# Two attention layers and four feed-forward passes on one core: q's and k's preparation cut into one-engine pieces, and begun earlier, with the next chunk's first row maxima moved to the end of chunk 0

## The chip, the core and the metric

One core of a Trainium2 chip. The metric is device time in microseconds (us) of one run of the whole program. Lower is better. Instructions run on TensorE (PE; its weight loads are shown as PEld), VectorE (DVE), ScalarE (ACT), GpSimd (POOL), and SyncE (SP), which here only issues DMAs. Each engine takes its own instructions strictly in the order in which the program lists them; semaphores make one wait for another.

## The reference: what is computed

The input x is 2048 positions by 256 features. A layer is x += 0.5 FFN(LN(x)); x += Attention(LN(x)); x += 0.5 FFN(LN(x)). There are two layers, so the stages are f0, attention 0, f1, f2, attention 1, f3, and each stage has its LayerNorm ahead. Layer 0's FFN has ternary weights and an RMS norm, layer 1's keeps the two largest of every four hidden values. Both attentions are causal, with 16 heads of 16 features:

```
q, k, v = LN(x) @ Wq, LN(x) @ Wk, LN(x) @ Wv         # layer 1: + bias
layer 1: q, k = q*cos + swap(q)*sin, k*cos + swap(k)*sin     # rotary
scores = q @ k^T / 4 (+ a position bias in layer 0), causal
x += softmax(scores) @ v @ Wo                        # layer 1: + bias
```

## The kernel before, in words

**Tiling.** x lies as features by positions, in four chunks of 512 positions (chunk c, `CH` = 512). A feed-forward stage goes through the chunks, and for each through eight hidden blocks f = 0..7 (L444 to L468): gate and up matmuls (`gate_up`, L281, or L306 in layer 0), Silu on ACT (L317), a product on DVE (L318), then in layer 1 the 2-of-4 choice (`sparsify`, DVE and POOL, L387 to L418) and the down matmuls (L292), which for a chunk are issued beside blocks 4 and 5 of the next chunk. After every block, `feed_forwards` calls `beside(s, at, f)` (L468), where `at` counts the chunks.

**Attention.** Heads go in four groups of four for each chunk of queries: group n = 4c + g. A *slot* is one pair (group n, key block kb of 128 keys); chunk c has 4(c+1) slots for each of its groups, so chunk 0 has slots 0 to 15, chunk 1 slots 16 to 47, chunk 2 slots 48 to 95. In a slot PE makes the transposed scores `pst` (L733, and the mask L741), ACT takes their exponential (L753, tile `pT`), and PE sums `pav` with the values (L768). The exponential needs the row maximum beforehand, folded into q as three more rows: so for a later group PE makes the scores the other way round, `pq` (L671, and the mask L679), and DVE reduces each to a maximum `mx` (L682). One *unit* (n, t, kc) is four such score blocks for 128 queries t against chunk kc of keys. When a group's units are done, `mx_end` (L689, L694) makes the negated maximum on DVE, and one slot later `mx_turn` (L699) transposes it on PE (`ptm`, L704), copies it on ACT (`qx`, L712) and stores it by three DMAs into three rows of the group's q tile (L714), for which that group's `pst` waits. PSUM has two pairs of banks for `pst`, and three single ones (`ps_one`) which `pq`, `pp`, `pv`, `ptm` share.

**Preparation.** `prep_qk(c, what)` (L521) is a generator; a *piece* runs from one yield to the next. It makes q or k of chunk c: matmuls `pp` for two halves (L536), in layer 0 a bf16 copy on ACT (L544) and the rest on DVE (L545), in layer 1 bias on ACT (L547, tile `dn`). Layer 1 then has the halves of `dn` swapped by two DMAs into `sw` (L556), multiplies `dn` by the cosine on DVE (L571) and `sw` by the sine on POOL (L575, two instructions), adds (DVE, L577), copies the bf16 part (ACT, L578) and subtracts it (DVE, L579). Both layers go on with the second part (ACT, L580) and third part (POOL, L581), and six DMAs to a scratch in DRAM (L585). Before the change, all of L577 to L585 is one piece. `prep_v` has two pieces of matmuls `pv` (L598) with the copies to `va` (ACT L609 in layer 0, DVE L611 in layer 1). `load` (L636) brings a group's k and q back from the scratch to SBUF (L640, L645).

**What sets the order.** There is no list scheduler for PE, ACT, DVE and POOL: they get their instructions in the order in which the Python code issues them. SP's DMAs are placed by a planner. Chunk 0's preparation is drawn from `beside0` and `beside1` (L1023, L1030), one piece a block, beside the last chunk of f0 and the last one and a half of f2. Chunk 1's is drawn by `step()` (L877) after each of the seven units ahead of slot 0 (the *opening*, L912 to L916), then once a slot; chunk c+1's, once a slot in chunk 1 and in every second slot in chunk 2 (L975). If a `load` wants what is not there, `need` (L880) draws all pieces up to it at once. `put` (L837) says in which slot a unit is issued (L846 to L859), `uses` and `load_to` (L900 to L908) load each group three slots ahead of its first unit.

Of the kernel before, what the change touches and what calls it, by code (L numbers as in the profile page):

```python
# [26 lines left out]
G = 4  # L27
F = 1024
FC = F // P
CH = 512  # L30
NCH = S // CH
# [15 lines left out]
def macaron_kernel(ctx: ExitStack, tc: tile.TileContext, a, out):  # L47
# [13 lines left out]
    def ps_one(name):  # L61
        return ps3.tile([P, CH], F32, tag="one", name=name)
# [124 lines left out]
    def draw(work):  # L187
        while work and next(work[0], "end") == "end":
            work.popleft()
# [7 lines left out]
    def ready(c):  # L197

        while pending[c]:
            pull()  # L200
# [289 lines left out]
    def attention(layer, following):  # L490
# [9 lines left out]
        with ExitStack() as st:  # L500
# [20 lines left out]
            def prep_qk(c, what):  # L521

                ready(c)
                if what == "k" and c > 0:
                    nc.gpsimd.memset(va[c], 1.0)
                at = 0 if what == "q" else DC
                name = f"{layer}_{what}{c}"
                dn = ka.tile([P, DC, CH], F32, tag="dn", bufs=2 - layer, name=f"dn{name}")
                pt = [
                    ka.tile([P, DC, CH], BF16, tag=f"part{j}", bufs=1, name=f"p{j}{name}")  # L530
                    for j in range(3)
                ]
                for i in range(DC):
                    pp = ps_one(f"pp{name}_{i}")
                    for dc in range(DC):
                        nc.tensor.matmul(  # L536
                            pp,
                            lhsT=wqkv[:, dc, (at + i) * P : (at + i + 1) * P],
                            rhs=xns[c][:, dc, :],
                            start=dc == 0,  # L540
                            stop=dc == DC - 1,
                        )
                    if layer == 0:
                        nc.scalar.copy(pt[0][:, i, :], pp)  # L544
                        nc.vector.tensor_tensor(dn[:, i, :], pp, pt[0][:, i, :], ALU.subtract)  # L545
                    else:
                        nc.scalar.activation(  # L547
                            dn[:, i, :], pp, AF.Identity, bias=b_qk[:, at + i : at + i + 1]
                        )
                    if i == 0:  # L550
                        yield
                if layer == 1:

                    sw = ka.tile([P, DC, CH], F32, tag="sw", bufs=1, name=f"sw_{what}{c}")
                    for o in range(2):
                        nc.sync.dma_start(  # L556
                            out=sw[o * 64 : o * 64 + 64, :, :],
                            in_=dn[64 - o * 64 : 128 - o * 64, :, :],
                        )
                    if turns.get("of") != c:  # L560
                        turns["of"] = c
                        turns["cs"] = ka.tile(
                            [P, 2, CH], F32, tag="cs", bufs=1, name=f"cs_{what}{c}"
                        )
                        nc.sync.dma_start(
                            out=turns["cs"], in_=a["cos_sin"][:, :, c * CH : (c + 1) * CH]
                        )
                    cs = turns["cs"]
                    yield
                    yield  # L570
                    nc.vector.tensor_tensor(  # L571
                        dn, dn, cs[:, 0:1, :].to_broadcast([P, DC, CH]), ALU.mult
                    )
                    for i in range(DC):
                        nc.gpsimd.tensor_tensor(sw[:, i, :], sw[:, i, :], cs[:, 1, :], ALU.mult)  # L575
                    yield
                    nc.vector.tensor_tensor(dn, dn, sw, ALU.add)  # L577
                    nc.scalar.copy(pt[0], dn)  # L578
                    nc.vector.tensor_tensor(dn, dn, pt[0], ALU.subtract)  # L579
                nc.scalar.copy(pt[1], dn)  # L580
                nc.gpsimd.tensor_tensor(pt[2], dn, pt[1], ALU.subtract)  # L581
                for j in range(3):
                    for m, part in enumerate(Q_PARTS if what == "q" else K_PARTS):
                        if part == j:
                            nc.sync.dma_start(  # L585
                                out=parts[what, c][:, m, :, :].rearrange("i p t -> p i t"),
                                in_=pt[j],
                            )
                done.add((what, c))
                yield  # L590

            def prep_v(c):
                ready(c)
# [24 lines left out]
            def first():  # L618
                nc.gpsimd.memset(va[0], 1.0)
                yield  # L620
                for work in (prep_qk(0, "k"), prep_qk(0, "q"), prep_v(0)):
                    yield from work
# [207 lines left out]
            first = []  # L830
# [3 lines left out]
            LEAD = 3  # L834
            maxima = {}

            def put(slot, n, t, kc):  # L837
                maxima.setdefault(max(slot, -1), []).append((n, t, kc))

            def whole(n):  # L840

                return [(n, t, kc) for kc in range(n // G) for t in range(T)] + [(n, 3, n // G)]
# [8 lines left out]
            for c in range(NCH):  # L851
                units = [u for n in groups[c * G + 1 : (c + 1) * G + 1] for u in whole(n)]
                places = [i for i, (n, kb) in enumerate(slots) if n // G == c and kb <= c * T]
                if c == 0:
                    places = range(first[G] - LEAD)
                if c == NCH - 1:
                    places = [i for i in places if slots[i][0] < groups[-1]]
                for j, u in enumerate(units):
                    put(places[j * len(places) // len(units)], *u)  # L859
# [7 lines left out]
            def run_due(all_of=False):  # L867
                while True:
                    due = [x for x in later if all_of or x[0] <= now[0]]
                    if not due:  # L870
                        return
                    later.remove(due[0])
                    due[0][1](*due[0][2])
# [3 lines left out]
            def step():  # L877
                draw(preps)
# [11 lines left out]
            def mx_next(unit, heads):  # L890
                n, t, kc = unit
                mx_unit(n, t, kc, heads)
                if 3 in heads:
                    left[n] -= 1
                    if not left[n]:
                        mx_end(n)
                        at(1, mx_turn, n)
# [11 lines left out]

            load_to(-1)  # L910
            preps.extend((prep_qk(1, "k"), prep_qk(1, "q"), prep_v(1)))
            for unit in maxima[-1]:  # L912
                mx_next(unit, (0, 1, 2, 3))
                step()
                now[0] += 1
                run_due()  # L916

# [21 lines left out]
            for i, (n, kb) in enumerate(slots):  # L939
                c = n // G  # L940
                if kb == 0 and n % G == 0 and 0 < c < NCH - 1:

                    preps.extend((prep_qk(c + 1, "k"), prep_qk(c + 1, "q"), prep_v(c + 1)))
# [3 lines left out]
                units = maxima.get(i, [])  # L947
# [69 lines left out]
    begun = []  # L1017

    def begin(layer, following):
        att = attention(layer, following)  # L1020
        begun[:] = att, next(att)

    def beside0(s, at, f):  # L1023
        if not quants and not begun:
            raw_scope.close()
            begin(0, "f1")
        if at == NCH - 1:
            next(begun[1], None)

    def beside1(s, at, f):  # L1030
        if s == 1 and at == 0 and f == FC // 2:
            own.close()
            ffn0_scope.close()
            begin(1, "f3")
        if s == 1 and (at == NCH - 1 or at == NCH - 2 and f >= FC // 2):
            next(begun[1], None)

    def attend():
        att, first = begun
# [15 lines left out]
    attn_w = {0: load_attn(0)}  # L1055
    w1 = None
    feed_forwards([(0, "f0", range(NCH))], beside0)
    attend()
    attn_w[1] = load_attn(1)
# [5 lines left out]
    w1 = (wgu1, wd1)  # L1065
# [5 lines left out]
    own = ExitStack()  # L1071
    own0 = own.enter_context(tc.tile_pool(name="own0", bufs=1, side="right"))
    feed_forwards([(0, "f1", range(NCH)), (1, "f2", range(NCH))], beside1, own0)
    attend()
    feed_forwards([(1, "f3", range(NCH))], lambda s, at, f: None)
# [95 lines left out]
```

## Time and profile before

| what | us |
|---|---|
| runs | 1935.06, 1936.63, 1938.12 (median 1936.63) |
| the profiled execution | 1938.73 (its span 1936.7) |
| PE busy | 1735.6 (90%) |
| DVE, ACT, POOL busy | 1353.1 (70%), 884.7 (46%), 456.9 (24%) |
| f2's last down matmul ends, attention 1's first `pq` starts | 1161.8, 1168.1 |
| first `pst` of chunk 0, 1, 2, 3 in attention 0 | 267.1, 323.1, 442.8, 606.2 |
| the same in attention 1 | 1196.1, 1267.2, 1397.5, 1568.2 |

The lines of the profile give start, duration, engine, source line, operation, output<-inputs and shapes; in brackets the time for which the engine stood idle just before, and what ended it. The rows by stretch give, for each engine, its busy time and in brackets its number of instructions, in the order PE, PEld, DVE, ACT, POOL, then the granted PE clock (1.00 is full, 0.50 half), the share of the DMA engines, and GB/s. The first `pst` of a chunk is found by counting: each slot has four L733 matmuls, an attention 160 slots.

### The profile page before, as it was taken

To read this page: it belongs to the slowest core of one execution; us is meant where nothing else is said; L and a number is where in the kernel's file an instruction comes from. 1 tells how busy PE (TensorE), PEld (TensorE's weight loads), DVE (VectorE), ACT (ScalarE), POOL (GpSimd) and SP (SyncE) were. 2 spreads that over 40 slices of the span, in tenths; PEclk is the share of its full clock that TensorE was granted. 3 is DMA by queue.
4 is the path that set the end of the run, shared out by engine and by line. 5 is a ranking of instruction groups with operands and counts; after the bars stand their busy time and mean duration, and the time that the engine had idled before them with its cause. 6 is when DMAs were issued, how large, how long until landed. Compare 5 with 4: busy or idle time off the path is not lost. (4 is left out here: it accounts for less than half of the span.)

```text
span 1936.7 us, 26968 instructions
## 1 busy us (share of the span) xinstructions
PE 1735.6 (90%) x10659; PEld 747.2 (39%) x10684; DVE 1353.1 (70%) x2384; ACT 884.7 (46%) x1112; POOL 456.9 (24%) x418
## 2 busy tenths in 40 slices
PE   5699788999999999789999875888998999999997
PEld 1233344443434443233444332433434344433443
DVE  7866378787788883666566655867867888826654
ACT  4243244555556668334432312444555656673220
POOL 3455321101000000455444432211111000004322
PEclk9799899999999999989999987998999999999998
DMA  4001252212211010200000115323122110000000
GB/s 130 1 1 33 79 154 72 85 55 82 74 55 46 28 28 1 74 1 0 1 12 0 54 44 153 104 73 97 52 70 87 43 43 27 18 2 0 11 11 22
DMA packets 50511, 93.10 MB, mean 48 GB/s; under 512 B 5425, under 2 KB 33073, under 8 KB 50129
## 3 DMA queue, kind: packets, MB, share of 16 engines
q1 hardware_dynamic: 49296, 89.28, 15.3%
q10 hardware_dynamic: 1088, 2.10, 0.3%
q8 instruction: 84, 1.38, 0.3%
q14 instruction: 43, 0.34, 0.1%
HBM read 59.51 MB, written 27.26 MB: 45 GB/s over the span
## 5 line engine op out<-in xcount | busy, mean ns | idle before, releaser
L682 DVE TENSOR_REDUCE mx<-pq 128x1 f32<-128x512 f32 (+3 forms) x1280 | 697.6, 602 | 146.0 <-PE pq L679 86.8
L753 ACT ACTIVATE pT<-pst 128x1024 f32<-128x1024 f32 (+3 forms) x614 | 533.1, 895 | 319.9 <-PE pst L733 166.4
L671 PE MATMUL pq<-k,q 105*128 105x512 bf16 (+7 forms) x1280 | 386.9, 351 | 76.9 <-DVE mx L682 55.3
L733 PE MATMUL pst<-q,k 99*128 99x512 bf16 (+7 forms) x1280 | 354.9, 351 | 5.1 <-ACT pT L753 4.3
L768 PE MATMUL pav<-pT,va 128*32 128x256 f32 (+1 forms) x4608 | 326.2, 379 | 5.2 <-DVE yt L789 5.0
L281 PE MATMUL pg_f<-xn,wgu 128*128 128x512 f32 x512 | 229.6, 602 | 11.5 <-DVE hr_f L318 11.5
L794 POOL TENSOR_TENSOR zt<-yt,rd 128x64 f32<-128x64 f32 x128 | 38.3, 299 | 774.4 <-DVE rd L793 774.3
L733 PEld LDWEIGHTS <-k 105*128 105x128 bf16 (+1 forms) x1280 | 111.0, 98 | 229.4 <-issue 165.2
L317 ACT ACTIVATE sl_f<-pg_f 128x512 f32<-128x512 f32 x128 | 76.0, 594 | 251.2 <-PE pg_f L281 174.9
L671 PEld LDWEIGHTS <-q 105*128 105x128 bf16 (+1 forms) x1280 | 124.0, 99 | 146.8 <-issue 44.3
L768 PEld LDWEIGHTS pav<-pT,va 128*32 128x32 f32 x4608 | 106.6, 109 | 190.9 <-issue 136.1
L306 PE MATMUL pg_f<-xn,wgu 128*128 128x512 bf16 x500 | 154.0, 413 | 20.8 <-DVE wgu L170 6.8
L281 PEld LDWEIGHTS pg_f<-xn,wgu 128*128 128x128 f32 x512 | 98.6, 193 | 136.9 <-issue 121.0
L306 PEld LDWEIGHTS <-wgu 128*128 128x128 bf16 x768 | 77.3, 101 | 167.1 <-issue 73.1
L292 PE MATMUL po_f<-h_f,wd 128*128 128x512 f32 x256 | 117.4, 613 | 17.3 <-DVE h_f L418 17.3
L340 POOL TENSOR_TENSOR ss_f<-ss_f,sq_f 128x512 f32<-128x512 f32 x56 | 90.5, 1615 | 110.7 <-ACT sq_f L339 110.5
L679 PE MATMUL pq<-mask_qk,ident_b 128*128 128x128 bf16 x512 | 107.0, 226 | 0.0
L741 PE MATMUL pst<-mask_kq,ident_b 128*128 128x128 bf16 x512 | 102.7, 221 | 0.0
L318 DVE TENSOR_TENSOR h_f<-sl_f,pg_f 128x512 f32<-128x512 f32 x64 | 43.6, 681 | 77.4 <-ACT sl_f L317 76.9
L306 PE MATMUL pg_f<-xm_f,wgu 128*128 128x512 bf16 x253 | 83.4, 411 | 14.8 <-DVE xm_f L238 14.3
L789 DVE STREAM_TRANSPOSE yt<-pav 128x128 f32<-128x128 f32 x128 | 39.7, 310 | 76.8 <-PE pav L768 76.8
L394 DVE TENSOR_TENSOR ge_f<-h_f 128x1536 bf16<-128x1536 f32 (+2 forms) x48 | 67.6, 1437 | 28.0 <-ACT h_f L387 28.0
(132 smaller groups left out, 1798.3 us busy)
## 6 DMA issues: line engine op xcount, KB each, us to landing
k<-dk SPq DMA_DIRECT2D x80, 384.0 KB
dk<-p_k SPq DMA_DIRECT2D x48, 256.0 KB
dq<-p_q SPq DMA_DIRECT2D x48, 256.0 KB
q<-dq SPq DMA_DIRECT2D x32, 384.0 KB
x<-in_xT ACTq DMA_DIRECT2D x4, 512.0 KB
raw<-in_w_gu SPq DMA_DIRECT2D x8, 256.0 KB
wgu<-in_w_gu SPq DMA_DIRECT2D x1, 2048.0 KB
cs_k<-in_cos_sin SPq DMA_DIRECT2D x4, 512.0 KB
```

Source lines behind the costliest of these rows:

```text
L281: nc.tensor.matmul(pg[:, half, :], lhsT=wgu[:, dc, half * F + f * P : half * F + (f + 1) * P], rhs=xn[:, dc, :], start=dc == 0, stop=dc == ...
L292: nc.tensor.matmul(po, lhsT=w[:, f, dc * P : (dc + 1) * P], rhs=h[:, f, :], start=f == 0, stop=f == FC - 1,)
L306: nc.tensor.matmul(pg[:, half, :], lhsT=wgu0[:, dc, half * F + f * P : half * F + (f + 1) * P], rhs=xp[part][:, dc, :], start=part == 0 an ...
L317: nc.scalar.activation(sl, pg[:, 0, :], AF.Silu)
L340: nc.gpsimd.tensor_tensor(ss, ss, sq, ALU.add)
L671: nc.tensor.matmul(pq, lhsT=qs[n][0:rows, hh, t * P : (t + 1) * P], rhs=ks[n, kc][0:rows, hh, 0:w], start=True, stop=kc < c,)
L679: nc.tensor.matmul(pq[:, w - P : w], lhsT=ident_b, rhs=mask_qk, start=False, stop=True)
L682: nc.vector.tensor_reduce(mxs[n][:, t, hh, kc : kc + 1], pq, AX.X, ALU.max)
L733: nc.tensor.matmul(ps[i][:, lo:CH], lhsT=ks[n, kc][0:rows, hh, t * P : (t + 1) * P], rhs=qs[n][0:rows, hh, lo:CH], start=True, stop=kc < c,)
L741: nc.tensor.matmul(ps[i][:, lo : lo + P], lhsT=ident_b, rhs=mask_kq, start=False, stop=True)
L753: nc.scalar.activation(pT[:, :, lo:CH], pair[:, :, lo:CH], AF.Exp, scale=0.25)
L768: nc.tensor.matmul(acc[hh * SLOT : (hh + 1) * SLOT, a:b], lhsT=va[kc][:, t, v0 : v0 + SLOT], rhs=pTs[hh // 2][:, hh % 2, a:b], start=kb == ...
```

## The change

It cuts `prep_qk` at four more places (a piece then holds instructions of one compute engine, save for the multiply with POOL's two and the copy with POOL's subtraction), and drops its last yield, so that the six DMAs to the scratch run in one call with the next generator's first piece. Chunk 0's preparation is begun four blocks earlier in f0 as well, and in f2's last chunk two pieces are drawn a block. In layer 1's opening, two pieces are drawn after each unit. In chunk 0, a group's last unit goes to the first slot of the group before it, and the five units of group 4 that were spread from slot 4 on come to slots 9 to 13.

```diff
--- before.py
+++ after.py
@@ -575,10 +575,14 @@
                         nc.gpsimd.tensor_tensor(sw[:, i, :], sw[:, i, :], cs[:, 1, :], ALU.mult)
                     yield
                     nc.vector.tensor_tensor(dn, dn, sw, ALU.add)
+                    yield
                     nc.scalar.copy(pt[0], dn)
+                    yield
                     nc.vector.tensor_tensor(dn, dn, pt[0], ALU.subtract)
+                yield
                 nc.scalar.copy(pt[1], dn)
                 nc.gpsimd.tensor_tensor(pt[2], dn, pt[1], ALU.subtract)
+                yield
                 for j in range(3):
                     for m, part in enumerate(Q_PARTS if what == "q" else K_PARTS):
                         if part == j:
@@ -587,7 +591,6 @@
                                 in_=pt[j],
                             )
                 done.add((what, c))
-                yield
 
             def prep_v(c):
                 ready(c)
@@ -852,7 +855,10 @@
                 units = [u for n in groups[c * G + 1 : (c + 1) * G + 1] for u in whole(n)]
                 places = [i for i, (n, kb) in enumerate(slots) if n // G == c and kb <= c * T]
                 if c == 0:
-                    places = range(first[G] - LEAD)
+
+                    for j, u in enumerate(units):
+                        put(first[u[0] - 1] if u[0] < G else first[G - 1] - 6 + j, *u)
+                    continue
                 if c == NCH - 1:
                     places = [i for i in places if slots[i][0] < groups[-1]]
                 for j, u in enumerate(units):
@@ -911,7 +917,8 @@
             preps.extend((prep_qk(1, "k"), prep_qk(1, "q"), prep_v(1)))
             for unit in maxima[-1]:
                 mx_next(unit, (0, 1, 2, 3))
-                step()
+                for _ in range(1 + layer):
+                    step()
                 now[0] += 1
                 run_due()
 
@@ -1020,20 +1027,25 @@
         att = attention(layer, following)
         begun[:] = att, next(att)
 
+    def go_on(at, f):
+        if at == NCH - 1 or at == NCH - 2 and f >= FC // 2:
+            next(begun[1], None)
+            if w1 and at == NCH - 1:
+                next(begun[1], None)
+
     def beside0(s, at, f):
         if not quants and not begun:
             raw_scope.close()
             begin(0, "f1")
-        if at == NCH - 1:
-            next(begun[1], None)
+        go_on(at, f)
 
     def beside1(s, at, f):
         if s == 1 and at == 0 and f == FC // 2:
             own.close()
             ffn0_scope.close()
             begin(1, "f3")
-        if s == 1 and (at == NCH - 1 or at == NCH - 2 and f >= FC // 2):
-            next(begun[1], None)
+        if s == 1:
+            go_on(at, f)
 
     def attend():
         att, first = begun
```

Line numbers after the change: up to L577 as before; the copy, the subtraction, the second copy and POOL's subtraction come to L579, L581, L583 and L584, the DMAs to the scratch to L589; from there to the placing of units three more (L598, L671, L682, L714, L733 and L768 become L601, L674, L685, L717, L736 and L771).

## Prediction

> **What bounds the kernel.** I read the page first: PE is busy 90% of the span, and PE has the largest share of the chain of waits (29%, DVE 6%), so time goes only where PE stops or runs at a lower clock. The two strips by slice show where that is; slices are 48.4 us.
>
> ```profile
> PE   5699788999999999789999875888998999999997
> ...
> PEclk9799899999999999989999987998999999999998
> ```
>
> The low digits in the body are slices 23 to 28, from f2's end (1114 us) to attention 1's chunk 1: the stretch that the change is about. Next, the rows by stretch, cut at the first `pst` of each chunk: attention 0's chunks 1 and 2, then attention 1's opening and chunks 0, 1 and 2.
>
> ```profile
> 323.10:442.80 119.70, 112.77 (x912) 49.37 (x909) 93.20 (x200) 64.91 (x82) 14.95 (x23) 1.00 0.23 71
> 442.80:606.20 163.40, 156.97 (x1292) 66.62 (x1288) 130.20 (x260) 92.83 (x110) 9.96 (x19) 1.00 0.22 68
> 1161.80:1196.10 34.30, 22.63 (x84) 11.27 (x83) 17.66 (x37) 4.72 (x6) 6.64 (x4) 0.70 0.56 156
> 1196.10:1267.20 71.10, 55.92 (x498) 29.92 (x496) 56.57 (x136) 35.34 (x48) 18.38 (x24) 0.93 0.35 101
> 1267.20:1397.50 130.30, 118.34 (x912) 50.93 (x908) 100.64 (x206) 66.38 (x80) 19.82 (x27) 0.95 0.26 75
> 1397.50:1568.20 170.70, 158.61 (x1293) 67.54 (x1290) 135.74 (x266) 94.06 (x108) 15.71 (x23) 0.99 0.21 64
> ```
>
> Both attentions have the same matmuls, yet chunk 1 lasts 130.3 us in layer 1 against 119.7, chunk 2 170.7 against 163.4. PE idles 12.0 and 12.1 us there against 6.9 and 6.4, and its busy time is 5.6 and 1.6 us longer at a clock of 0.95 and 0.99. What layer 1 has more is the rotary. The timeline shows it, in layer 1's slots 0 and 1, where `need` draws q's whole preparation at once:
>
> ```profile
> 1201.56 1.23 DVE L571 TENSOR_TENSOR dn_q<-dn_q,cs_k 128x1024 f32<-128x1024 f32 x1 [1.29 <-DMA sw_q<-dn_q]
> 1205.16 1.23 DVE L577 TENSOR_TENSOR dn_q<-dn_q,sw_q 128x1024 f32<-128x1024 f32 x1 [2.37 <-POOL sw_q L575]
> 1207.54 1.23 DVE L579 TENSOR_TENSOR dn_q<-dn_q,p_q 128x1024 f32<-128x1024 f32 x1 [1.16 <-ACT p_q L578]
> ...
> 1209.29 0.48 PE L671 MATMUL pq<-k,q 99*128 99x384 bf16 x1 [8.14 <-DVE mx L682]
> ```
>
> DVE waits for the swap's DMAs, for POOL and for ACT, and the `mx` behind it in DVE's order leave no free PSUM bank: PE stands 8.14 us. In chunk 1 k's joined piece does it on a smaller scale:
>
> ```profile
> 1296.39 1.23 DVE L579 TENSOR_TENSOR dn_k<-dn_k,p_k 128x1024 f32<-128x1024 f32 x1 [1.11 <-ACT p_k L578]
> ...
> 1298.14 0.32 PE L671 MATMUL pq<-k,q 99*128 99x384 bf16 x1 [2.12 <-DVE mx L682]
> ```
>
> **Part by part**, against the profiled execution (1938.73 us, 2.1 over the runs' median 1936.63).
>
> *f0.* k's matmuls come four blocks earlier, ahead of the split on which chunk 3's first matmuls wait:
>
> ```profile
> 165.36 0.61 PE L306 MATMUL pg_f<-xm_f,wgu 128*128 128x512 bf16 x2 [2.20 <-DVE xm_f L238]
> ...
> 166.69 1.80 PE L306 MATMUL pg_f<-xn,wgu 128*128 128x512 bf16 x4 [0.73 <-DVE xn L239]
> ```
>
> Idle 2.93, and the clock was half from 166.8 to 170.2 (1.7 lost). Two halves of `pp` (1.88 each, by L536's rows) move to where they cover the wait, but bring two L545 (0.69 each) onto DVE ahead of it: 3.76 − 1.38 = 2.4 of the 2.93. I take −2.5; ends 0 (DVE merely later) and −4 (with the clock).
>
> *Attention 0.* Opening: one more piece for each generator, all of it ACT, POOL and DMAs beside units: 0. Chunk 0: group 4's maximum is now finished one slot before slot 16, so `ptm`, `qx` and its three DMAs begin with slot 15:
>
> ```profile
> 743.13 0.39 PE L704 MATMUL ptm<-ident_b,neg 128*12 128x128 bf16 x4
> ...
> 744.15 1.83 SPq L714 DMA_DIRECT2D q<-qx  x3
> ...
> 747.23 1.02 PE L733 MATMUL pst<-q,k 105*128 105x512 bf16 x4 [0.35 <-DMA q<-qx]
> ```
>
> That is 4.1 us from `ptm` to `pst`; slot 15 lasts 2.2, so 1.9 of wait. The five units in slots 9 to 13 crowd DVE by 0.7 (one maximum of L682, 0.60 on average), and the emptier slots ahead lose about 1 of idle (a gap of 1.50 at 284.4). +1.6; I take +1.5, from −3 (nothing waits, all idle goes) to +4 (the wait in full, and another group's).
>
> *f2.* Before, k's joined piece lay in chunk 3's first blocks and q's last piece in f7. Now the multiply and the add are one block's, adjacent on DVE; the add has POOL's two (2.93) and four other POOL operations before it, and behind it wait the products for the next `pg` and down matmuls. PE waited 5.88 for `hr_f` there; I take about 7. Against this, ACT is free in f7, where `sl_f` stood behind two copies:
>
> ```profile
> 1139.24 0.69 DVE L318 TENSOR_TENSOR hr_f<-sl_f,pg_f 128x512 f32<-128x512 f32 x1 [1.61 <-ACT sl_f L317]
> ```
>
> With the copies' 1.05 each, about −2.4; and v's second piece no longer covers the stage's end, +0.7 (a gap of 4.64 before the first `pq` loses its filler). So −2.4 + 1.1 + 0.7 = −0.6, which I take; ends −4 (the add costs no more than before, and the down matmuls that wait for `h_f` later gain too) and +2 (ACT's time in f7 was hidden).
>
> *Layer 1's opening and chunk 0.* Two pieces a unit, so that the multiply comes one unit after the swap was issued. The swap took 4.3 us and 4.4 us from issue to landing, one unit covers about 1.4; DVE holds 3, works 1.23, and PE stands about 4, once for k, once for q. But q's preparation is through by slot 2 without force, since group 4's first load moves from slot 1 to slot 6. Idle before, from the first `pq` (1168.1) to slot 2 (1216.8): 2.00 + 0.75 + 3.37 + 0.90 + 8.14 = 15.2. After: 2.0 + 4 + 4.5 = 10.5. So −5, and v's two pieces, drawn by force before slot 2 before, now lie in slots 2 and 3: +2. The rest of chunk 0 as in attention 0 (+1.6). I take −1.4; ends −8 (no new half clock) and +14 (below).
>
> *Attention 1, chunk 1.* k and most of q in pieces, one a slot; only q's last copy and its DMAs are still drawn by force, at slot 31. Slots give 2.2 to 2.8 us between pieces against ACT's 1.04 and POOL's 2.1, so DVE no longer waits in mid-preparation: the gaps 1.91, 2.12 and 1.71 shrink to about 2.4 less in all; and if PE doesn't pause, the 5.6 of half clock go. One more piece in the last slots, +1. I take −7; ends −10 (layer 0's 119.7) and +1.
>
> *Chunk 2.* Pieces in every second slot; the forced rest (copy, subtraction, copy with POOL, DMAs) begins at slot 75, three slots ahead of use: 1.04 + 1.23 + 1.04 + 2.1 and the way through the scratch, some 13.5 against about 13.3 of time; 0 to 2 of stall. Gaps of 2.57 and 2.18 go, 1.6 of clock perhaps. I take −3; ends 0 and −7.
>
> Sum: −2.5 + 1.5 − 0.6 − 1.4 − 7 − 3 = −13.0: 1925.7 for the profiled execution, **1923.6** against the median.
>
> [...] The clock falls to half in stretches of 3.4, 6.8 or 10.2 us. The two in chunk 1 follow gaps of at most 2.1 us:
>
> ```profile
> 1312.00:1317.10 5.10, 2.73 (x10) 0.89 (x10) 5.07 (x9) 2.05 (x2) 2.74 (x3) 1.00 0.18 65
> 1317.10:1327.30 10.20, 8.98 (x47) 3.24 (x47) 7.96 (x13) 4.04 (x4) 2.14 (x1) 0.50 0.60 194
> ```
>
> The upper row is q's forced preparation: PE busy 2.73 of 5.1 us, in several gaps, none over 1.71; the lower is what followed. I read it as thin work, not one long gap, that costs the clock, and thin work is what the pieces remove. [...]
>
> **Rivals.**
> - *The clock stays.* What lowers it in chunks 1 and 2 isn't the joined pieces. For it: 1.91 and 2.12 at 1290 and 1298 brought no fall. Against: it fell in no such place of attention 0, at 1.00 throughout. −13.0 + 5.6 + 1.6 = −5.8: 1930.8 (all rivals' times against the median).
> - *Layer 1 becomes like layer 0.* Chunks 1 and 2 lose the whole difference, −10.6 and −7.3 for −7 and −3: −20.9, 1915.7. Against: DVE still has 7.4 us more work in chunk 1 (100.64 against 93.20).
> - *It doesn't do what it says.* The change's order still has forced draws at slots 31 and 75; if these, not k's pieces, make the gaps and the half clock, chunks 1 and 2 gain nothing: −3.0, 1933.6.
> - *Slower: DVE held in the opening.* Swap and multiply, multiply and add stand one unit apart, so DVE waits for the DMAs and then for POOL, as it did in slot 1; each of k and q costs the 8.14 of that place instead of some 4, and PE runs at half clock throughout, as it did from 1204.4 to 1214.7 behind the 8.14. In that stretch PE is busy 32.6 us at a mean clock of 0.70, so about 22.8 at full and 45.7 at half clock (an estimate from that row); with idle of 2 + 8.14 + 8.14 that is 64.0 for 48.7: +15.3 instead of −3. Another 10.2 us at half in the slots behind: +5.1. In all −13.0 + 18.3 + 5.1 = +10.4: 1947.0. It decides when the stretch from the first `pq` to slot 2 exceeds some 63 us. Against it: more units lie between the pieces than in slot 1, where there were none.
>
> **Chances.** Forecast 0.40 (its own range 1918 to 1929), clock stays 0.22, as layer 0 0.13, not done 0.10, slower 0.15. The range, 1911 to 1941, takes in the rivals' centres but the slower one's, and leaves out some 0.2 (most of the slower case and the outer ends of the others). A change of 0.2% (3.9 us) is about what a measurement of this kernel can tell from none. Faster by more: 0.36 of the forecast, 0.15 of the clock case, 0.13, 0.03: 0.67; within: 0.03 + 0.06 + 0.05 + 0.03 = 0.17; slower: the rest, 0.16.
>
> **What would show it.** Chunk 1 of attention 1 from first `pst` to first `pst`: 123 if right, over 128 if the pieces gain nothing; its clock 1.00 or 0.95. Chunk 2: 167.7. Group 4's first `pst` waits on `qx` 1.9 us in both layers. From the first `pq` of attention 1 to slot 2: 45. Chunk 3's first `pg` in f0 waits under 1 us on the split; f2's `pg` about 7 on `hr_f`. I am wrong if the opening's two holds bring long half clock, or if PE in chunk 1 waits for something other than DVE's order.

## The result and the profile after

The changed kernel takes 1929.56 us (median of 5 runs, 1926.89 to 1931.97), the kernel before, run beside it, 1938.12 (1935.06 to 1940.51). The ratio is 0.9954, with a 95% interval of 0.9940 to 0.9969: 9 us faster, where I had forecast 13. The profiled execution takes 1931.97 us, 6.8 less than that of before, with a span of 1930.1, 6.6 less. The strips by slice of the changed kernel, as they were shown of the one before:

```profile
PE   5699788999999999879999885889999999999997
...
PEclk9799899999999999999999997999999999999998
```

Counted from 0 at the left, PE's digit has risen in slices 23 (f2's end) and 27 (attention 1's chunk 1, 1303 to 1351 us), in both of which the clock's digit has risen too, from 8 to 9; it has also risen in 16 and 30 and fallen in 17. Slice 24 (1158 to 1206 us) still has PE at 5 and the clock at 7, the lowest since the start. That slice is layer 1's opening. The rows by stretch, in the order of before (PE, PEld, DVE, ACT and POOL busy, granted clock, DMA share, GB/s), give the amounts: attention 0's chunks 1 and 2, then attention 1's opening from its first `pq`, and its chunks 0, 1 and 2.

```profile
322.10:442.90 120.80, 113.93 (x909) 49.86 (x910) 92.72 (x198) 64.96 (x82) 14.58 (x22) 0.99 0.23 70
442.90:605.80 162.90, 156.86 (x1292) 66.58 (x1288) 130.07 (x260) 93.04 (x110) 9.91 (x19) 1.00 0.22 68
1164.90:1199.90 35.00, 21.10 (x76) 10.19 (x77) 16.04 (x34) 5.32 (x7) 7.21 (x4) 0.70 0.56 151
1199.90:1269.10 69.20, 58.42 (x498) 31.20 (x496) 55.30 (x140) 35.00 (x47) 17.11 (x25) 0.92 0.29 87
1269.10:1392.50 123.40, 113.90 (x909) 49.67 (x910) 99.50 (x204) 65.99 (x80) 21.33 (x26) 0.99 0.27 79
1392.50:1561.30 168.80, 161.26 (x1293) 67.29 (x1290) 136.03 (x266) 94.10 (x108) 16.81 (x23) 0.97 0.21 65
```

Chunk 1 has become 6.9 us shorter: PE's idle time fell from 12.0 to 9.5, its busy time with the same matmuls from 118.34 to 113.90, and the clock is 0.99 for 0.95. The opening, from first `pq` to first `pst`, has grown from 28.0 to 35.0. All stages, by first `pq` and first `pst` (attention 0 is taken to end, and f1 to begin, at the first `pst` of its last slot), in the profiled executions:

| stage | before | after | change | forecast |
|---|---|---|---|---|
| start to first `pq` of attention 0 (f0) | 238.9 | 236.1 | −2.8 | −2.5 |
| first `pq` to chunk 1 | 84.2 | 86.0 | +1.8 | +1.5 |
| chunk 1, attention 0 | 119.7 | 120.8 | +1.1 | 0 |
| chunks 2 and 3 | 334.8 | 334.4 | −0.4 | 0 |
| f1, f2, to first `pq` of attention 1 | 390.5 | 387.6 | −2.9 | −0.6 |
| first `pq` to chunk 1 | 99.1 | 104.2 | +5.1 | −1.4 |
| chunk 1, attention 1 | 130.3 | 123.4 | −6.9 | −7 |
| chunk 2, attention 1 | 170.7 | 168.8 | −1.9 | −3 |
| the rest | 368.5 | 368.8 | +0.3 | 0 |

One row carries the largest miss: layer 1's opening with chunk 0. In the timeline of the changed kernel's opening (start, duration, engine, line; in brackets the idle time ahead):

```profile
1177.11 1.23 DVE L571 TENSOR_TENSOR dn_k<-dn_k,cs_k 128x1024 f32<-128x1024 f32 x1 [3.33 <-DMA sw_k<-dn_k]
...
1178.85 0.48 PE L674 MATMUL pq<-k,q 99*128 99x384 bf16 x1 [4.64 <-DVE mx L685]
...
1180.71 1.23 DVE L577 TENSOR_TENSOR dn_k<-dn_k,sw_k 128x1024 f32<-128x1024 f32 x1 [0.52 <-POOL sw_k L575]
...
1182.59 0.58 PE L674 MATMUL pq<-k,q 99*128 99x512 bf16 x1 [1.51 <-DVE mx L685]
```

The multiply waits 3.33 us for the swap's DMAs, and every `mx` behind it with it; PE stands 4.64. Then the add waits for POOL, and PE stands another 1.51. q does the same 21 us later, and there ACT's order adds a wait of its own:

```profile
1198.30 1.23 DVE L571 TENSOR_TENSOR dn_q<-dn_q,cs_k 128x1024 f32<-128x1024 f32 x1 [3.36 <-DMA sw_q<-dn_q]
...
1199.78 0.27 PE L674 MATMUL pq<-k,q 99*128 99x128 bf16 x1 [4.51 <-DVE mx L685]
...
1203.21 1.04 ACT L579 CAST p_q<-dn_q 128x1024 bf16<-128x1024 f32 x1 [9.43 <-DVE dn_q L577]
1204.27 1.28 ACT L756 ACT_TABLE_LOAD   x1
1205.56 1.94 ACT L756 ACTIVATE pT<-pst 128x1024 f32<-128x1024 f32 x2
...
1206.64 0.48 PE L736 MATMUL pst<-q,k 99*128 99x384 bf16 x1 [2.16 <-ACT pT L756]
```

q's copy stands ahead of slot 0's first exponential and waits for the held add; the load of the exponential's table (1.28) comes only behind the copy. PE's two pairs of `pst` banks stay full, 2.16 us. The end of the chunk shows the wait on `qx` that was forecast, in attention 0 and attention 1:

```profile
322.08 0.59 PE L736 MATMUL pst<-q,k 105*128 105x512 bf16 x2 [1.56 <-DMA q<-qx]
```
```profile
1269.12 0.60 PE L736 MATMUL pst<-q,k 99*128 99x512 bf16 x2 [1.44 <-DMA q<-qx]
```

And f2, whose end has gained more than forecast, first of the kernel before, then of the changed one:

```profile
1103.38 6.42 PE L281 MATMUL pg_f<-xn,wgu 128*128 128x512 f32 x8 [5.88 <-DVE hr_f L318]
...
1152.67 9.09 PE L292 MATMUL po_f<-h_f,wd 128*128 128x512 f32 x16 [10.25 <-DVE h_f L418]
...
1168.12 0.26 PE L671 MATMUL pq<-k,q 99*128 99x128 bf16 x1 [4.64 <-DMA q<-in_q_rows]
```
```profile
1098.03 1.22 PE L281 MATMUL pg_f<-xn,wgu 128*128 128x512 f32 x1 [5.96 <-DVE hr_f L318]
...
1149.29 1.19 PE L292 MATMUL po_f<-h_f,wd 128*128 128x512 f32 x1 [5.95 <-DVE h_f L418]
...
1164.89 0.27 PE L674 MATMUL pq<-k,q 99*128 99x128 bf16 x1 [6.41 <-DMA q<-in_q_rows]
```

### The profile page after: what moved, and what is told of

Same layout as the page of the kernel before. It is cut to its first block, busy times and chain, and to the rows that moved or that the text cites. A ratio compares the mean times of both kernels' runs of the same rounds, so it can differ in the third digit from the quotient of the medians.

```text
span 1930.1 us, 27004 instructions
## 1 busy us (share of the span) xinstructions
PE 1740.1 (90%) x10684; PEld 747.9 (39%) x10684; DVE 1345.2 (70%) x2384; ACT 884.3 (46%) x1110; POOL 461.4 (24%) x418
## 4 chain that ended last, share of the span: by engine, by line
PE 72%; DVE 19%; ACT 3%; issue 2%; POOL 2%; DMA 1%; SPq 0%; DVEq 0%; ACTq 0%; POOLq 0%
PE pav L771 14%; PE pst L736 12%; PE pq L674 10%; PE pg_f L281 10%; DVE mx L685 7%; PE pg_f L306 6%; PE po_f L292 5%; PE po_f L361 4%; PE pp_k L536 2%; PE pp_q L536 2%; PE pwo L812 1%; PE pv L601 1%; PE pst L744 1%; PE pq L682 1%; DVE h_f L329 1%
## 5 line engine op out<-in xcount | busy, mean ns | idle before, releaser
L685 DVE TENSOR_REDUCE mx<-pq 128x1 f32<-128x512 f32 (+3 forms) x1280 | 697.2, 602 | 151.0 <-PE pq L682 83.8
L674 PE MATMUL pq<-k,q 105*128 105x512 bf16 (+7 forms) x1280 | 388.2, 352 | 71.8 <-DVE mx L685 47.6
L736 PE MATMUL pst<-q,k 99*128 99x512 bf16 (+7 forms) x1280 | 358.3, 354 | 10.3 <-ACT pT L756 6.5
L771 PE MATMUL pav<-pT,va 128*32 128x256 f32 (+1 forms) x4608 | 325.2, 378 | 5.5 <-DVE yt L792 5.0
L736 PEld LDWEIGHTS <-k 105*128 105x128 bf16 (+1 forms) x1280 | 111.5, 98 | 231.4 <-issue 168.0
L674 PEld LDWEIGHTS <-q 105*128 105x128 bf16 (+1 forms) x1280 | 123.8, 99 | 148.9 <-issue 48.7
L771 PEld LDWEIGHTS pav<-pT,va 128*32 128x32 f32 x4608 | 106.3, 108 | 188.6 <-issue 133.8
L682 PE MATMUL pq<-mask_qk,ident_b 128*128 128x128 bf16 x512 | 106.4, 225 | 0.0
```

The lines of the kernel that those rows point to most:

```text
L674: nc.tensor.matmul(pq, lhsT=qs[n][0:rows, hh, t * P : (t + 1) * P], rhs=ks[n, kc][0:rows, hh, 0:w], start=True, stop=kc < c,)
L682: nc.tensor.matmul(pq[:, w - P : w], lhsT=ident_b, rhs=mask_qk, start=False, stop=True)
L685: nc.vector.tensor_reduce(mxs[n][:, t, hh, kc : kc + 1], pq, AX.X, ALU.max)
L736: nc.tensor.matmul(ps[i][:, lo:CH], lhsT=ks[n, kc][0:rows, hh, t * P : (t + 1) * P], rhs=qs[n][0:rows, hh, lo:CH], start=True, stop=kc < c,)
L771: nc.tensor.matmul(acc[hh * SLOT : (hh + 1) * SLOT, a:b], lhsT=va[kc][:, t, v0 : v0 + SLOT], rhs=pTs[hh // 2][:, hh % 2, a:b], start=kb == ...
```

## The experiments

Each was timed beside the kernel before. The stages of all of them, from the profiled executions: A is the way from first `pq` to chunk 1's first `pst` in attention 0, B f1 and f2 to attention 1's first `pq`, C as A in attention 1, D chunk 1 and E chunk 2 of attention 1.

| kernel | ratio to before (95%) | A | B | C | D | E |
|---|---|---|---|---|---|---|
| before | 1 | 84.2 | 390.5 | 99.1 | 130.3 | 170.7 |
| after | 0.9954 (0.9940 to 0.9969) | 86.0 | 387.6 | 104.2 | 123.4 | 168.8 |
| e1 units back | 0.9917 (0.9900 to 0.9933) | 86.2 | 384.3 | 98.9 | 126.8 | 166.8 |
| e2 pieces only | 0.9978 (0.9968 to 0.9988) | 86.4 | 398.1 | 97.1 | 123.8 | 168.2 |
| e3 open one | 0.9894 (0.9876 to 0.9912) | 85.9 | 387.6 | 90.7 | 123.4 | 168.0 |
| e4 begin late | 1.0002 (0.9993 to 1.0012) | 86.0 | 396.0 | 102.3 | 123.7 | 166.5 |
| e5 group 4 sooner | 0.9905 (0.9891 to 0.9919) | 83.5 | 387.4 | 96.8 | 122.2 | 166.7 |
| e6 spread | 0.9901 (0.9887 to 0.9915) | 85.6 | 384.3 | 94.5 | 123.4 | 168.0 |
| e7 chunk 2 joined | 0.9981 (0.9972 to 0.9990) | 85.7 | 386.9 | 104.4 | 128.7 | 166.8 |
| e8 open some | 0.9921 (0.9907 to 0.9935) | 85.7 | 386.9 | 96.3 | 125.4 | 167.7 |
| e9 layer-wise | 0.9860 (0.9845 to 0.9876) | 84.8 | 382.7 | 95.1 | 123.8 | 167.1 |
| e10 sooner, drawn | 0.9875 (0.9861 to 0.9890) | 85.4 | 387.1 | 95.1 | 123.8 | 166.5 |
| e11 q joined | 0.9958 (0.9945 to 0.9971) | 85.6 | 386.6 | 104.5 | 126.4 | 167.0 |

B shows what one profile is worth: ten of these kernels have the changed kernel's program there, and it took 382.7 to 387.6 us. A, which is shorter, took 85.6 to 86.0 in the six kernels with the changed kernel's program there, but 83.5, 84.8 and 85.4 in e5, e9 and e10, which have one program there among them. So a difference of 2 us in one stage of one profile need not be the edit's. PE's idle time in B varies by 2.4 us in these ten (41.4 to 43.8), B itself by 4.9; the rest is PE's busy time. What half clock does to that, e1 shows: in attention 0's slots 0 to 15 PE was busy 52.35 us with 3.4 us at half clock, in the changed kernel 51.20 with none.

**e1: chunk 0's units where they were.**

```diff
                 if c == 0:
-                    for j, u in enumerate(units):
-                        put(first[u[0] - 1] if u[0] < G else first[G - 1] - 6 + j, *u)
-                    continue
+                    places = range(first[G] - LEAD)
```

> The changed kernel, with chunk 0's units put in their slots as before the change. Theory: the change lost most of what I forecast too much in chunk 0, where group 4's five units crowd slots 9 to 13 (DVE busy 26.2 of 29.8 us there in attention 0, and 1.5 us of wait on qx at slot 16). Then chunk 0 of attention 0 goes from 59.9 back to about 56 us, chunk 0 of attention 1 from 69.2 to about 66, the waits on qx vanish, and the time is some 7 us below the changed kernel: about 1922.5. Rival: chunk 0 is longer for the pieces of preparation that now lie in it; then both stay within 1 us of 59.9 and 69.2, and the time stays at about 1929.

Measured: 1923.97 us. The time came out about as expected; the theory's way was half right. In attention 1 chunk 0 fell from 69.2 to 63.7, more than the theory's 66, and C by 5.3 (idle time from 24.7 to 20.2), less 3.4 that chunk 1 lost to 10.2 us of half clock. In attention 0 the waits on `qx` vanished too, but A did not move (86.2). The rows of attention 0's slots 0 to 8 and 9 to 15 show why, first of the changed kernel, then of e1:

```profile
262.20:292.30 30.10, 27.78 (x264) 15.68 (x263) 23.50 (x62) 22.73 (x32) 8.78 (x13) 1.00 0.41 117
292.30:322.10 29.80, 23.42 (x227) 11.83 (x226) 26.20 (x69) 10.37 (x17) 3.04 (x9) 1.00 0.30 75
```
```profile
261.30:300.70 39.40, 33.26 (x280) 17.62 (x279) 33.04 (x77) 22.93 (x32) 8.50 (x13) 0.96 0.39 111
300.70:321.60 20.90, 19.09 (x209) 10.28 (x208) 18.07 (x52) 10.16 (x17) 3.03 (x8) 1.00 0.23 67
```

The units' time moves between the halves (30.1 and 29.8, or 39.4 and 20.9) and the sum stays. PE's idle time in them falls from 8.70 to 7.95, but e1's first row has 3.4 us of half clock (at 282.1), and PE's busy time is 1.15 longer. Neither row of either kernel has DVE over 0.88 busy.

**e2: the cuts alone.** `prep_qk` of the changed kernel in the kernel before, nothing else.

> The kernel before, with nothing but the new cuts in q's and k's preparation: begun, drawn and placed as before. Theory: chunks 1 and 2 of attention 1 become as in the changed kernel (123.4 and 168.8 us, within 1.5), but since chunk 0's preparation now has more pieces than blocks beside which they are drawn, its end stands ahead of attention 1 with nothing beside it, and q of chunk 1 is again drawn by force: the way from f2's end to chunk 1 is 10 to 15 us longer, and the time is about 1938 plus or minus 4. Rival: the cuts alone bring the whole gain: 1930, and the other edits nothing.

Measured: 1934.39. D and E are those of the changed kernel (123.8 and 168.2), so the cuts alone are what shortens them; A is about the changed kernel's too (86.4), but for another reason: about 1.6 of the 2.2 us over the kernel before are PE's busy time, with 3.4 us of half clock at 285.2. e1, which has the same cuts and the same placing, has that fall at the same place, 21 us after the first `pst`; the kernel before and the changed kernel do not have it. B is 10.5 longer than in the changed kernel: the rest of chunk 0's preparation stands alone ahead of attention 1, where PE idles 13.86 us before the first `pq`. C is shorter than expected, 97.1, though q is drawn by force there with 10.17 us of idle PE, since the opening took only 20.2 us: the whole way to chunk 1 (B and C) is 5.6 longer than before and not 10 to 15.

**e3: one piece a unit in the opening.**

```diff
-                for _ in range(1 + layer):
-                    step()
+                step()
```

> The changed kernel, with one piece after each unit of layer 1's opening, as before the change. Theory: the two stops of PE of 4.64 and 4.51 us in the opening come from the multiply standing one unit behind the swap; with one piece a unit they go, first pq to first pst falls from 35.0 to about 28 us, and the forced draw of q's rest at slot 6 costs 3 to 5 us: the time falls by about 3, to 1926.5. Rival: the forced draw costs as much as in the kernel before (8 us of idle PE), and the time is 1931 to 1934.

Measured: 1916.84, about 12 us below the changed kernel and not 3. The way from first `pq` to chunk 1 in attention 1, of the changed kernel and of e3:

```profile
1164.90:1269.10 104.20, 79.52 (x572) 41.38 (x572) 71.35 (x172) 40.31 (x54) 24.32 (x28) 0.84 0.38 108
```
```profile
1165.40:1256.10 90.70, 76.08 (x572) 40.09 (x572) 71.93 (x172) 40.09 (x54) 24.10 (x28) 0.89 0.46 124
```

The same 572 matmuls: idle time falls from 24.7 to 14.6 us, busy time by 3.4 at a clock of 0.89 for 0.84. The opening is 20.2 us for 35.0; slots 2 to 15, which now hold q's pieces and the forced rest, are 4.4 longer. I had priced the forced draw right (slot 5 lasts 9.0 us, in the changed kernel 4.5) and the second piece's cost at half.

**e4: begun as late as before.** `beside0` and `beside1` draw one piece a block, in the last chunk of f0 and the last twelve blocks of f2.

> The changed kernel, with chunk 0's preparation drawn beside the feed-forward as before the change (one piece a block: chunk 3's in f0, the last twelve blocks in f2). Theory: what is left of it at the stage's end is done with nothing beside it; f0 and the opening of attention 0 lose the 5 us that they gained (first pst at 267 again), f2 and the opening of attention 1 lose 5 to 8 more: about 1940. Rival: that preparation is hidden in either place, and the time is within 2 us of the changed kernel's.

Measured: 1940.00, as expected: the whole gain of the change is gone. B is 8.4 longer, with 13.63 us of idle PE before attention 1's first `pq`, f0 3.5.

**e5: group 4's units one slot sooner, one piece a unit in the opening.** `first[G - 1] - 6 + j` becomes `- 7 + j`, with e3's edit.

> The changed kernel with one piece a unit in the opening and group 4's five units one slot sooner (slots 8 to 12). Theory: the waits of 1.5 us on qx at slot 16 come from finishing group 4 one slot before it; they vanish in both attentions, and the rest of chunk 0 stays as with one piece a unit (59.9 and 70.6 us): about 3 us below that kernel's 1916.8, 1914. Rival: slots 9 to 15 are paced by DVE (26.2 of 29.8 us busy), and the wait on qx only stood where PE would have waited for DVE anyway: chunk 0 within 0.5 us of 59.9, 1916.8.

Measured: 1919.77, no better than e3. In attention 0 the wait on `qx` went, and chunk 0 lasts 58.9 us for 59.9 (in e9 too): the wait's worth is 1.0. A fell further, to 83.5, but the rest of that is the opening, with a clock of 0.90 for 0.82; e9 and e10, with the same program there, have 84.8 and 85.4. In attention 1 the load in slot 5 comes one slot before q is ready for it, and the draw by force brings back the picture of before in one piece, C 96.8:

```profile
1204.57 1.23 DVE L577 TENSOR_TENSOR dn_q<-dn_q,sw_q 128x1024 f32<-128x1024 f32 x1 [2.62 <-POOL sw_q L575]
1206.95 1.23 DVE L581 TENSOR_TENSOR dn_q<-dn_q,p_q 128x1024 f32<-128x1024 f32 x1 [1.15 <-ACT p_q L579]
...
1208.89 0.50 PE L674 MATMUL pq<-k,q 99*128 99x384 bf16 x1 [6.70 <-DVE va L614]
```

**e6 and e8: two pieces after four of the seven units,** so that a multiply comes two units behind its swap; e6 also spreads group 4's units.

```diff
-            for unit in maxima[-1]:
+            for j, unit in enumerate(maxima[-1]):
...
-                for _ in range(1 + layer):
+                for _ in range(2 if layer and j in (0, 3, 4, 5) else 1):
```

> The changed kernel with two pieces only after units 0, 3, 4 and 5 of layer 1's opening, so that each multiply comes two units behind its swap, and q is still begun in the opening. Theory: what the two pieces cost was DVE held for the swap, 4.6 and 4.5 us of PE's idle time and the half clock behind it; without these the way from the first pq to the first pst of chunk 1 falls from 104.2 to about 92 us, within 2 us of one piece a unit (90.7): 1918. Rival: it is q's matmuls, bias and swap in the opening themselves, at half clock and with nothing beside them; then it is 98 or more: 1924.

Measured: 1921.99, C 96.3. k's multiply now waits 1.43 us (for 3.33), q's 1.51 (for 3.36), and PE stands 2.83 and 3.38 at them. That took 7.9 of the 13.5 us that lie between the changed kernel and e3. What is left, 5.6, is no more than the 6.2 us for which PE still stands at the two multiplies, so the rival, that q's work in the opening costs by itself, is not shown; nor is it excluded.

> The changed kernel with two pieces only after units 0, 3, 4 and 5 of layer 1's opening, and group 4's units in slots 7, 8, 10, 12 and 12. Theory: DVE's load is even over chunk 0's slots, nothing waits for qx, and q of chunk 1 is ready without force: chunk 0 of attention 0 falls by 3 from 59.9, and the way from the first pq to the first pst of chunk 1 in attention 1 (104.2 in the changed kernel, 90.7 with one piece a unit) to about 87: 1911. Rival: the pieces in the opening cost what they cost wherever they stand, 95 or more there: 1920.

Measured: 1918.69, C 94.5, A 85.6, near the rival's 95 and 1920 and not the theory's 87 and 1911. Nothing waits on `qx` any more at slot 16. In A PE's idle time fell from 12.7 to 11.0, but its busy time rose by 1.4, with 3.4 us of half clock at 297.2.

**e7: chunk 2's preparation in layer 1 joined,** so that joined pieces lie beside chunk 1 only. The new yields are under `if not (layer == 1 and c == 2)`, and the old last one is back for that case.

> The changed kernel, with chunk 2's q and k of layer 1 prepared in joined pieces as before the change: they lie beside chunk 1 of attention 1. Theory: the joined pieces leave gaps of PE, and the thin work costs the clock; chunk 1 of attention 1 goes from 123.4 back to about 130 us, with 10 us of half clock near its middle, everything else as in the changed kernel: 1936. Rival: the fall of the clock in the kernel before was not theirs; then only 2.4 us of idle time come back, chunk 1 is 126 with 3.4 us of half clock: 1932.

Measured: 1934.44; D is 128.7 for 123.4, and the picture of the kernel before is back to the gap: PE waits 1.94, 2.12 and 1.71 us at 1289.7, 1297.3 and 1316.6, and then the clock is half for 10.2 us.

```profile
1311.20:1316.30 5.10, 2.70 (x10) 0.86 (x9) 5.07 (x9) 2.05 (x2) 2.75 (x3) 1.00 0.17 62
1316.30:1326.50 10.20, 9.01 (x47) 3.27 (x47) 7.92 (x13) 4.04 (x4) 2.14 (x1) 0.50 0.60 195
```

So with the joined preparation the clock fell, in both profiles at the same place (50 and 48 us after chunk 1's first `pst`). But this is also where I misread the profile before: what lies in the thin stretch is not q's forced preparation. It is slot 24, with two units of maxima, and q's multiply behind them on DVE:

```profile
1314.37 1.62 DVE L571 TENSOR_TENSOR dn_q<-dn_q,cs_k 128x1024 f32<-128x1024 f32 x1
...
1316.64 0.59 PE L680 MATMUL pq<-k,q 99*128 99x512 bf16 x1 [1.71 <-DVE mx L691]
```

DVE is busy 5.07 of 5.10 us there. With k in pieces the multiply falls to a later slot.

**e11: q alone joined,** k in pieces: the joined piece is there, and q's multiply is in slot 27.

> The changed kernel, with chunk 2's q alone of layer 1 prepared in a joined piece; its k stays in pieces, so q's multiply falls to slot 27 and not to slot 24, which has two units of maxima. Theory: the 10.2 us of half clock in chunk 1 belong to the multiply in the slot with the most work for DVE, not to the joined piece; the clock holds, and chunk 1 of attention 1 is 124 to 126 us: 1931. Rival: the joined piece itself costs the clock: about 10 us of half clock near slot 28, chunk 1 at 128 or more: 1934.

Measured: 1931.41, D 126.4. The long half clock does not come back (3.4 us only), the joined piece's own wait does:

```profile
1327.78 1.22 DVE L583 TENSOR_TENSOR dn_q<-dn_q,p_q 128x1024 f32<-128x1024 f32 x1 [1.11 <-ACT p_q L580]
1329.53 0.32 PE L680 MATMUL pq<-k,q 99*128 99x384 bf16 x1 [2.45 <-DVE mx L691]
```

So the 10.2 us of half clock in before and e7 come with the multiply in the slot that has the most maxima; the joined piece costs its 2.45 us of wait. (e7 has k joined as well, but the fall comes 19 us behind k's wait and right behind q's multiply.) That the cuts avoided this fall is a matter of which slot each piece fell to, not of their being cut. Nor do the cuts exclude a fall: in the ten profiles with all pieces cut, chunk 1 has from 0 (e5) to 10.2 us (e1) at half clock.

**e9 and e10: the draw that follows from e3 and e5.** Both have one piece a unit in the opening. e9 has group 4 sooner in attention 0 alone and draws two pieces in attention 1's slots 0 and 4; e10 has it sooner in both, with two pieces in slots 0, 1 and 3.

```diff
                 if preps and (c <= 1 or i % 2):
                     step()
+                    if layer and i in (0, 4):
+                        step()
```

> The changed kernel with one piece a unit in layer 1's opening, group 4's units one slot sooner in attention 0 alone, and in attention 1 two pieces in slots 0 and 4. Theory: in attention 0 the wait on qx goes (59.9 to 58.9 or less, as with group 4 sooner), and in attention 1 q's copy and subtraction no longer fall to the forced draw ahead of slot 6, where slot 5 took 9.0 us: from the first pq to the first pst of chunk 1, 90.7 falls to about 87. In all some 5 below the kernel with one piece a unit: 1912. Rival: the forced draw only moves work and slots 9 to 15 take back what slot 5 gives: 90 there, 1916.

Measured: 1912.76, the fastest of all. But the theory's step is not what did it: C is 95.1 and not 87 (2.61 us of wait for group 4's q from the scratch at 1217.0, and 10.2 us at half clock from 1216.6). What is better than in e3 in this profile is A (−1.1), chunk 1 of attention 0 (119.4 for 120.8) and B (−4.9), and B is the same program. How far e9 is really ahead of e3 stays open: their intervals, 0.9845 to 0.9876 and 0.9876 to 0.9912, only meet.

> The changed kernel with one piece a unit in layer 1's opening, group 4's units one slot sooner in both attentions, and in attention 1 two pieces in slots 0, 1 and 3, so that only q's last copy and its DMAs are left for the load ahead of slot 5. Theory: with group 4 sooner the forced draw in slot 5 cost 14.2 us (6.7 of PE's idle time) against 9.0; without it the way from first pq to the first pst of chunk 1, 97.0 there, falls to about 87, and no wait on qx is left: 1911. Rival: the multiply, now one slot behind its swap, holds DVE again: 93 or more, 1918.

Measured: 1917.41, C 95.1 (96.8 in e5): the forced draw's 6.70 us are gone, the rest of the theory did not come. The rival's 93 and 1918 did, but its hold is small: the multiply waits 1.28 us for its swap and PE 1.42; another 2.37 us PE waits for `mx` at 1226.4. e3 keeps the shortest C.

## Why the prediction was right, and where it was not

- **f0** (−2.5, measured −2.8): the 2.20 us wait on the split and the half clock at 166.8 are gone.
- **Attention 0 to chunk 1** (+1.5, measured +1.8): right. PE's idle time rose by 1.3 and its busy time by 0.5. The wait on `qx` was forecast at 1.9 and is 1.56; taking it away brings 1.0 (e5, e9). With the units where they were, chunk 0 idles 0.75 less (e1), and a fall of the clock, not the amount of work, keeps A at 86 there. Chunk 1 then has 3.4 us of half clock, which I did not forecast, +1.1; it is not in e4, e5 and e9.
- **f2** (−0.6, measured −2.9). `pg`'s wait of 5.96 was forecast at 7, the last down matmul's fell from 10.25 to 5.95, where I had counted 2.4, and the first `pq`'s rose by 1.8, from 4.64 to 6.41, where I had 0.7. The stage's time in one profile says little, with B's spread of 4.9; but PE's idle time there is 41.4 to 43.8 us in all ten profiles of the new program and 46.2 in the one of before, so 2.4 to 4.8 of it are gone, and the forecast was too small. That the earlier start is worth some 8 us once the pieces are cut, e4 shows.
- **Layer 1's opening and chunk 0** (−1.4, measured +5.1). This is the step that failed: "After: 2.0 + 4 + 4.5 = 10.5. So −5". The two holds were sized right, 4.64 and 4.51; left out were the add's wait for POOL (1.51) and slot 0's exponential behind q's copy on ACT (2.16), so that PE's idle time ahead of slot 2 is 16.1 us as before, and the stretch to slot 2 is 47.6 us and not 45. Slots 2 to 15 then take 56.6 for 50.4, where I had 3.6 more: PE's busy time is 3.7 longer there, at full clock in both, since one of v's pieces and one unit now lie behind slot 2 and not ahead of it, and idle time is 2.5 longer. Worse, the step asked the wrong question. I weighed two pieces against the forced draw of before; the alternative was one piece, since the later load had already left of that draw only q's rest. e3 shows the doubled step's price: 12 us. The slower rival had this mechanism in the right place, and its full price did not come: 47.6 is far from its 63.
- **The two edits in that stretch** depend on each other, and I had priced each alone. By one profile each, C with one piece a unit is 97.1 us with the units where they were (e2, whose chunk 0 is prepared later) and 90.7 with them moved (e3); with two pieces it is 98.9 (e1) and 104.2 (the changed kernel). So moving the units gains 6 us with one piece and loses 5 with two.
- **Chunk 1** (−7, measured −6.9): right, in both terms, 2.5 of idle time for 2.4 and 4.4 of busy time for 5.6; e7 brings back 5.3 of it. The idle time's part is the cuts': 9.5 to 9.7 us in all ten profiles with cut pieces, 12.0 or 12.1 in before, e7 and e11. The clock's part came true by luck: thin work, yes, but DVE's multiply in a crowded slot, not a forced or joined piece (e11), and among the ten profiles the chunk took 122.2 to 126.8. The row from 1312.0 that the prediction calls q's forced preparation is that slot. Of the rivals, *The clock stays* did not come.
- **Chunk 2** (−3, measured −1.9): the gaps of 2.57 and 2.18 are gone and idle time fell by 4.6, but there are 10.2 us of half clock for 3.4, and busy time rose by 2.7. In e4, e5 and e10, with the same pieces, the chunk took 166.5 to 166.7.

So 9 us came of a forecast gain of 13. Between the profiles the gain is 6.6, and the miss of 6.5 in layer 1's opening and chunk 0 is as large as the whole shortfall; that is partly luck, since the other misses (f2 −2.3, chunk 1 of attention 0 and chunk 2 of attention 1 +1.1 each) cancel.

## What to carry to other kernels

Cutting a chain over several engines into pieces of one engine pays only with enough other work between the pieces: price each distance against the latency that it must cover (here 4.5 us from the swap's issue at 1172.64 to k's multiply at 1177.11, against one unit of 1.4, and DVE stood 3.33), and look at every engine's queue behind the piece, ACT's too. When an edit removes a forced draw, ask anew whether the edits made against that draw are still wanted; undoing one of them (e3) was worth more than the whole change. Where two edits move work within one stretch, price them together: here one of them changed sign with the other. Count what stands in a slot on the engine that is fullest there, before blaming the piece that is longest.

## What the runs showed of the hardware

In two places of attention 1 the changed kernel's clock fell though no gap of PE just ahead was as long as 1 us. In chunk 1 the only fall is at 1372.0; the row ahead of it and the fall itself, and the same ahead of a fall in chunk 2 at 1484.6:

```profile
1368.60:1372.00 3.40, 2.23 (x9) 0.77 (x8) 3.37 (x8) 0.74 (x2) 0.29 (x1) 0.99 0.26 67
...
1481.20:1484.60 3.40, 1.81 (x12) 0.46 (x12) 3.37 (x8) 0.88 (x1) 3.09 (x4) 1.00 0.05 17
```
```profile
1372.00:1375.40 3.40, 3.40 (x15) 0.79 (x13) 2.60 (x5) 1.36 (x2) 0.00 (x0) 0.50 0.00 0
```

PE was busy 2.23 and 1.81 of 3.4 us there, DVE 3.37, and the longest single gap was 0.64 and 0.93 us. In the profiles of before and after, the 3.4 us ahead of every fall within the attentions' slots had PE busy at most 0.66 (at 1372.0 and 1443.6 in the changed kernel), and ahead of e7's fall at 1316.3 it was 0.55; but 0.55 from 1477.5 to 1480.9 in before had no fall behind it, so this busy share is not the whole condition. The falls in the profiles of before and after lasted 3.4, 6.8, 10.2 or 13.7 us (in before at 166.8, 1102.0, 1317.1 and 235.1), save the last of each, which the profile's end cuts. Where the falls lie differs between kernels with the same slots (103 us after the first `pst` of chunk 1 in the changed kernel, 23 in e4, 40 in e9), as far as only one 3.4 us stretch is concerned, but the same few places come back: 103 in e3 and e6 too, 40 to 41 in e2 and e10. The 10.2 us in one piece came at 50 us in before and at 48 in e7.
